# Attention's value product copied out of its accumulator bank by ScalarE, and its PSUM banks shared out anew

## The chip, the cores and the metric

The kernel runs on one core of a Trainium2 chip. The engines are named as in the profile: PE (TensorE; PEld are its weight loads), DVE (VectorE), ACT (ScalarE), POOL (GpSimd) and SP (SyncE, which here only issues transfers). The metric is the device time of one execution in microseconds (us); lower is better. "Clock" is the share of full speed that TensorE was granted.

## The reference, cut to what matters

One post-norm transformer block over x of shape (2, 1024, 512), fp32:

```
q, k, v = split heads of x @ W.T + b + 0.5 * (x @ B.T) @ A.T     # 16 heads of 32, rank 16
attn    = softmax(q @ k.T * 32**-0.5)                            # per batch and head, 1024 x 1024
x       = layernorm(x + lora_linear(attn @ v; Wo, bo, Bo, Ao))
out     = moe(x)      # softmax gate, the best of 8 experts, capacity 256, hidden 704, SwiGLU
shared  = (silu(x @ sw1) * (x @ sw3)) @ sw2
x       = layernorm(x + out + shared)
```

## The kernel before, in words

fp32 products on TensorE are made from a high and a low part (a value cast to a shorter type, and what the cast left out), so that most products consist of three.

The kernel has four stages: the projections (0 to 156 us of the profile), attention (156 to 600), the output projection of the second batch with the shared feed-forward part, and the experts (to 1043). The change lies in attention.

Attention is cut into 16 units u: four heads (of one batch) by half of the queries, so g = u // 2 is the group of four heads. A unit has eight steps, one for each block of 128 keys; step t = 8u + k. The lines below are those of the profile.

- `st_step(t)`: four score matmuls st (L641), one for each head, keys on the partitions, into banks of the PSUM pool `one` (three banks). ACT turns each into an exponential (L650) in a tile pt of SBUF, two heads in one tile of 128 x 1024; the pool `ptp` has PTB of these tiles. After each head stands a list, `between[h]`, of other work.
- `maxima()` makes one of the row maxima that the softmax of a unit needs 12 steps later (LEAD): a matmul s (L203) into a bank of the pool `s1p`, and a DVE reduction of it (L211). The table `S_AT[k][h]` says how many are put into list h of step k, ahead of the other work and behind it. `finish_max` transposes a unit's maxima (L221 mp; ACT L224, DVE L225) and sends them into the tile of queries, where the score matmul subtracts them.
- `av_step(t)`: the product with the values, av (L660), eight steps accumulated in one PSUM bank of the pool `avp` (two banks, so units take turns). At every even t, in list AVQ = 3, stand the av of the two steps before: 16 matmuls. So unit u's last av stands at t = 8(u + 1).
- `adds(t-1)`: the pt tiles of a unit are added up, ahead of the row sums. The table ADDS names what is done at each k: "dd" an accumulating transfer issued by POOL (L678), "pp" additions on POOL, "vv" on DVE (both L681), two of 128 x 1024 each; "pp0" means that tile 0 is added. Units 14 and 15 use DVE.
- `finish(u)` (table FIN): matmuls with ones (L694 sm) give the sums in a bank, ACT copies them (L708 rc), and they go by transfers through DRAM into a small shape r16. `invert(u)` (REC): DVE's reciprocal (L718) and transfers that spread it to rb. Units 14 and 15 take DVE's reciprocal of the sums themselves (L704).
- `normalize(u)` (NRM): part 0, DVE multiplies av by rb in place (L733); part 1, the cast to the high part at_h, on ACT (L738), for units 13 and 14 on DVE (L736); part 2, DVE's low part at_l = av − at_h (L740). For an ordinary unit this stands in step 8(u + 2) + 1, and ends the use of the av bank.
- `add_res(n)` (RES_ADDS): POOL adds the output bias to a block of the residual (L749). `oproj` (OPROJ_AT, L766) is the output projection, of batch 0 between the steps, of batch 1 behind the loop; its first block `op10` takes a bank of `avp`, the others of `s1p` (OP_ONE).

Entries of FIN, REC and NRM are (units later, step k, list); NU − 3 is unit 13. PE, ACT, DVE, POOL and SP run in the order in which the loop issues their work. PSUM's eight banks are shared out as 3 (`one`) + 2 (`avp`) + 3 (`s1p`). The projections use the same pools: `bank1` takes three turns in `one` and one in `avp`, and `fold_w` three blocks in `s1p` and the fourth in `avp`.

Of the kernel before, what the change touches and what calls it, by code (L numbers as in the profile page):

```python
# [9 lines left out]
F32 = mybir.dt.float32  # L10
# [3 lines left out]
ALU = mybir.AluOpType  # L14
AX = mybir.AxisListType
PSUM = bass.MemoryType.PSUM
DRAM = bass.MemoryType.DRAM

P = 128
B, L, D = 2, 1024, 512  # L20
NU = 16
# [3 lines left out]
KC = D // P  # L25
# [5 lines left out]
EPS = 1e-5  # L31
NT = T // P
LEAD = 12
LATE, OP_ONE = (0,), 1
NS = NU * 8
WARM, WCOL = 4, 256
OPER = 4
PTB = 14
OHB = 3
LOADS = {  # L40
    (2, 0): (("k", 0),), (2, 1): (("q", 0),), (2, 3): (("q", 1),),
# [13 lines left out]
AVQ = 3  # L55


FIN = {None: (1, 4, 1), NU - 3: (1, 3, 1), NU - 2: (1, 2, 3)}
REC = {None: (1, 6, 3), NU - 3: (1, 5, 3)}
NRM = {  # L60
    None: ((2, 1, 0), (2, 1, 2), (2, 1, 2)),
    NU - 3: ((2, 0, 1), (2, 0, 1), (2, 0, 1)),
    NU - 2: ((1, 4, 1), (1, 4, 1), (1, 4, 1)),
}


S_AT = (
    ((0, 0), (0, 1), (1, 0), (1, 0)), ((0, 0), (0, 1), (1, 1), (0, 0)),
    ((0, 2), (1, 0), (0, 0), (0, 2)), ((0, 0), (0, 1), (0, 2), (0, 0)),
    ((0, 1), (1, 2), (0, 1), (1, 1)), ((1, 0), (0, 0), (2, 0), (1, 0)),  # L70
    ((0, 0), (1, 0), (0, 1), (1, 0)), ((0, 1), (1, 0), (0, 0), (2, 0)),
)
XTB = 2


ADDS = {
    None: {1: "bb1 dd21", 2: "dd30", 3: "pp4", 4: "pp5", 5: "pp6", 6: "pp0"},
    NU - 2: {1: "bb1 dd01", 3: "dd23 vv4", 4: "vv5", 5: "vv6 vv3", 6: "vv7"},
    NU - 1: {1: "bb1 dd01", 3: "dd23 vv4", 4: "vv5", 6: "vv3"},
}  # L80
OPROJ_AT = (66, 68, 70, 72, 74, 76, 78, 80)
RES_AT = tuple(8 * i + (2 if i % 2 else 6) for i in range(8)) + (70, 74, 86, 90, 100, 102, 106, 110)
RES_ADDS = tuple(t + 3 for t in RES_AT[:14]) + (119, 120)
RB = 2
BTB = 4
AHEAD = 5
# [26 lines left out]
def kernel(  # L113
# [3 lines left out]
    pe, act, dve, pool, sp = nc.tensor, nc.scalar, nc.vector, nc.gpsimd, nc.sync  # L117

    def f(ap):
        return ap.bitcast(F32)  # L120
# [23 lines left out]
    wop = att_right.enter_context(tc.tile_pool(name="wop", bufs=1, side="right"))  # L144
    one_ps = ExitStack()
    one = one_ps.enter_context(tc.tile_pool(name="one", bufs=3, space=PSUM))
    avp = one_ps.enter_context(tc.tile_pool(name="avp", bufs=2, space=PSUM))
    s1p = one_ps.enter_context(tc.tile_pool(name="s1p", bufs=3, space=PSUM))
    wo_h = wop.tile([P, KC, D], F32R, name="wo_h")
    wo_l = wop.tile([P, KC, D], F32R, name="wo_l")  # L150
    Ks = [stk.tile([98, 4, 1024], F32R, name=f"ks{i}") for i in range(2)]
# [11 lines left out]
    def load_k(g, cs=slice(0, 1024), hs=slice(0, 4)):  # L163
        kt = Ks[g % 2]
        for blk, hl in ((0, 0), (1, 1), (2, 0)):
            sp.dma_start(
                out=f(kt[32 * blk : 32 * blk + 32, hs, cs]),
                in_=qk_d[1, g // NG, g % NG, hl].rearrange("(h p) t -> p h t", p=32)[:, hs, cs],
            )
# [13 lines left out]
    def load_q(u, hs=slice(0, 4)):  # L183
        g, qb = u // 2, u % 2
        for blk, hl in ((0, 0), (1, 0), (2, 1)):
            sp.dma_start(
                out=f(Qs[u % 3][32 * blk : 32 * blk + 32, hs]),
                in_=qk_d[0, g // NG, g % NG, hl].rearrange("(h p) t -> p h t", p=32)[
                    :, hs, qb * 512 : qb * 512 + 512
                ],  # L190
            )

    mts, pts, avs, accs, vts = {}, {}, {}, {}, {}
# [40 lines left out]
    with ExitStack() as ph1, tc.manual_schedule(engines=MAN1):  # L234
# [49 lines left out]
            return ba  # L284

        def fold_w(i, ba, k):
            if k == KC - 1:
                lp = avp.tile([P, 512], F32, name=f"lp{i}{k}", tag="av")
            else:
                lp = s1p.tile([P, 512], F32, name=f"lp{i}{k}", tag="s1")  # L290
            pe.matmul(lp, ba[0][:, k * P : k * P + P], ba[1], start=True, stop=True)
            return lp

# [328 lines left out]
    with ph2, tc.manual_schedule(engines={mybir.EngineType.PE}):  # L622
        ptp = att_left.enter_context(
            tc.tile_pool(name="ptp", bufs=PTB, side="left", reuse_waits="tile")
        )
        ap = ph2.enter_context(
            tc.tile_pool(name="ap", bufs=1, side="right", reuse_waits="tile")
        )
# [25 lines left out]
        def av_step(t):  # L654
            u, kc = t // 8, t % 8
            g = u // 2
            if kc == 0:
                avs[u] = avp.tile([P, 512], F32, name=f"av{u}", tag="av")
            for h in range(4):
                pe.matmul(  # L660
                    avs[u][32 * h : 32 * h + 32, :],
                    vts[g][:, kc, 32 * h : 32 * h + 32],
                    pts[t, h // 2][:, h % 2, :],
                    start=kc == 0,
                    stop=kc == 7,
                    skip_group_check=True,
                )

        def adds(t):
            u, kc = t // 8, t % 8  # L670
            for op in ADDS.get(u, ADDS[None]).get(kc, "").split():
                i = u * 8 + int(op[2])
                for pr in range(2):
                    if op[pr] == "b":
                        accs[u, pr] = pts[i, pr]
                    elif op[pr] == "d":
                        to = u * 8 + int(op[3])
                        pool.dma_start(out=pts[to, pr], in_=pts[i, pr], accum_op=ALU.add)  # L678
                    else:
                        eng = dve if op[pr] == "v" else pool  # L680
                        eng.tensor_tensor(accs[u, pr], accs[u, pr], pts[i, pr], ALU.add)  # L681
# [4 lines left out]
        fin = {}  # L686
# [41 lines left out]
        def normalize(u, parts=(0, 1, 2)):  # L728
            g, qb = u // 2, u % 2
            cs = slice(qb * 512, qb * 512 + 512)  # L730
            hi, lo = at_h[:, g % NG, cs], at_l[:, g % NG, cs]
            if 0 in parts:
                dve.tensor_tensor(avs[u], avs[u], fin[u], ALU.mult)  # L733
            if 1 in parts:
                if u in NRM_DVE:
                    dve.tensor_copy(hi, avs[u])  # L736
                else:
                    act.copy(hi, avs[u])  # L738
            if 2 in parts:
                dve.tensor_tensor(lo, avs[u], f(hi), ALU.subtract)  # L740

        def load_res(n):
            b, i = divmod(n, 8)
# [35 lines left out]
        def run(gen):  # L779
            for _ in gen:  # L780
                pass
# [12 lines left out]
        def at_step(table, t, q):  # L794
            for v in range(max(t // 8 - 2, 0), t // 8):
                at = table.get(v, table[None])
                at = at[q] if isinstance(at[0], tuple) else at
                if (v + at[0]) * 8 + at[1] == t:
                    yield v

        for t in range(NS):
            u, k = t // 8, t % 8
            if k == 0:

                if u % 2 == 0 and 2 <= u and u // 2 + 1 < B * NG:
                    for hs in (slice(0, 2), slice(2, 4)):
                        load_k(u // 2 + 1, hs=hs)
                        load_q(u + 2, hs)
                elif u >= 1 and u + 2 < NU:
                    load_q(u + 2)  # L810
                if u % 2 and NG <= u // 2 + 1 < B * NG:
                    load_v(u // 2 + 1)
            if t in RES_AT:
                load_res(RES_AT.index(t))
            between = [[], [], [], []]
            for q in range(4):
                between[q] += [maxima] * S_AT[k][q][0]
            if t + LEAD == NS:
                between[AVQ].append(lambda: finish_max(NU - 1))

            if t and t % 2 == 0:
                between[AVQ].append(lambda: (av_step(t - 2), av_step(t - 1)))
            for v in at_step(FIN, t, 0):
                between[FIN.get(v, FIN[None])[2]].append(lambda v=v: finish(v))
            for q in range(4):
                between[q] += [maxima] * S_AT[k][q][1]
            if t:
                between[AVQ].append(lambda: adds(t - 1))
            for q in range(3):
                for v in at_step(NRM, t, q):  # L830
                    between[NRM.get(v, NRM[None])[q][2]].append(lambda v=v, q=q: normalize(v, (q,)))
            for v in at_step(REC, t, 0):
                if v < RDIR:
                    between[REC.get(v, REC[None])[2]].append(lambda v=v: invert(v))
            if t in RES_ADDS:
                between[3].append(lambda: add_res(RES_ADDS.index(t)))

            if t in OPROJ_AT:
                op0 = oproj(0, OPROJ_AT.index(t), OPER)
                for q in range(3):  # L840
                    between[q].append(lambda q=q, op0=op0: run(op0) if q == 2 else next(op0))
            st_step(t, between)
            for _, fn in [x for x in later if x[0] == 0]:
                fn()
            later[:] = [(n - 1, fn) for n, fn in later if n]
            if t - NS >= OPROJ1:
                next(op10, None)
# [511 lines left out]
```

## Time and profile before

| | before |
|---|---|
| median of 3 runs | 1047.83 us (1046.94 to 1050.71) |
| the profiled execution | 1045.05 us |
| its span, first to last instruction | 1043.3 us |
| mean granted clock of TensorE | 0.991 |
| instructions on PE, DVE, ACT, POOL | 5606, 1156, 985, 404 |
| busy 165 to 563 us (398 long): PE, DVE, ACT, POOL | 396, 316, 258, 337 us |
| busy 576 to 589 us (13 long): PE, DVE, ACT, POOL | 8.4, 7.5, 4.4, 1.5 us; clock 0.74 |

In a row of the timeline stand the start, the duration from first start to last end (a row can hold several instructions, "x8"), the engine, the line, the operation with its tiles, and in brackets the idle time of the engine ahead of it with what released it. In a group's row, busy time and the mean duration in nanoseconds of one instruction stand behind the bar, then the idle time. DMA issues are rows of POOL and SPq. The ends of matmuls are modelled; their starts are recorded.

### The profile page before, as it was taken

What the parts mean: (1) busy time and instruction counts of PE and PEld (TensorE: products, weight loads), DVE (VectorE), ACT (ScalarE), POOL (GpSimd) and SP (SyncE); (2) the same over time, 40 slices, a digit from 0 to 9 for tenths busy, and PEclk for the clock granted to TensorE, in tenths of its full rate; (3) what the DMA queues carried; (4) which work ended last, traced back from release to release, by engine and by line L of the source; (5) the groups of instructions that cost most, each with busy time, mean ns of one, the idle gap of its engine ahead of it and who ended that gap; (6) DMA issues with size and microseconds to landing.
All of it is one profiled execution on the core that took longest, in us unless ns stands there. A gap on an engine that the chain in (4) does not pass through costs nothing. (4 is left out here: it accounts for less than half of the span.)

```text
span 1043.3 us, 15652 instructions
## 1 busy us (share of the span) xinstructions
PE 1016.6 (97%) x5606; PEld 722.7 (69%) x5606; DVE 676.1 (65%) x1156; ACT 520.4 (50%) x985; POOL 536.1 (51%) x404
## 2 busy tenths in 40 slices
PE   8999999999999999999999799999999999999994
PEld 6888784544444456654444279988788899999994
DVE  7732788788878877788877774222253467777752
ACT  5422206666666656576666645222132356555662
POOL 4000006889888977879895155000006056666674
PEclk9999999999999999999999899999999999999998
DMA  9876875686868783587974532000109667777721
GB/s 291 283 230 210 248 211 118 125 186 137 190 134 187 160 181 83 115 168 155 197 163 92 132 104 70 22 21 1 40 1 293 212 198 237 255 244 258 224 82 60
DMA packets 87374, 164.75 MB, mean 158 GB/s; under 512 B 15944, under 2 KB 24648, under 8 KB 87296
## 3 DMA queue, kind: packets, MB, share of 16 engines
q1 hardware_dynamic: 74240, 117.59, 38.8%
q0 software_dynamic: 13056, 46.16, 19.9%
q8 instruction: 44, 0.72, 0.3%
q14 instruction: 34, 0.28, 0.1%
HBM read 96.10 MB, written 33.80 MB: 125 GB/s over the span
## 5 line engine op out<-in xcount | busy, mean ns | idle before, releaser
L211 DVE TENSOR_REDUCE mt<-s 128x1 f32<-128x512 f32 x512 | 318.4, 681 | 75.2 <-PE s L203 75.1
L650 ACT ACTIVATE pt<-st 128x512 f32<-128x512 f32 x512 | 266.3, 618 | 147.5 <-PE st L641 145.6
L681 POOL TENSOR_TENSOR pt<-pt,pt 128x1024 f32<-128x1024 f32 x112 | 264.2, 2387 | 33.4 <-DMA pt<-pt 18.1
L203 PE MATMUL s<-ks,qs 96*128 96x512 f32 x512 | 196.1, 416 | 1.5 <-DVE mt L211 1.0
L641 PE MATMUL st<-qs,ks 98*128 98x512 f32 x512 | 189.3, 417 | 2.7 <-ACT pt L650 1.7
L678 POOL DMA_DIRECT2D pt<-pt x64 | 56.3, 1008 | 195.2 <-PE s L203 164.7
L641 PEld LDWEIGHTS st<-qs,ks 98*128 98x128 f32 x512 | 94.8, 189 | 72.5 <-ACT pt L650 26.8
L203 PEld LDWEIGHTS s<-ks,qs 96*128 96x128 f32 x512 | 94.2, 188 | 72.7 <-DVE mt L211 44.5
L924 PE MATMUL h<-xthe,w13s 128*128 128x256 f32 x704 | 129.9, 283 | 0.0
L924 PEld LDWEIGHTS h<-xthe,w13s 128*128 128x128 f32 x704 | 110.6, 191 | 0.4
L924 PE MATMUL h<-xtle,w13s 128*128 128x256 f32 x352 | 100.2, 285 | 0.0
L912 POOL TENSOR_TENSOR w2s<-w2r,w2s 128x512 fp32r<-128x512 f32 x42 | 65.8, 1588 | 64.9 <-ACT w2s L911 56.3
L1114 POOL DMA_INDIRECT xd_d<-x1a,slot_i x8 | 7.9, 985 | 139.3 <-DVE slot_i L1111 137.2
L660 PE MATMUL av<-pt,vt 128*32 128x512 f32 x512 | 64.0, 613 | 4.3 <-DVE at_l L740 4.3
L924 PEld LDWEIGHTS h<-xtle,w13s 128*128 128x128 f32 x352 | 67.3, 191 | 0.7
L660 PE MATMUL av<-pt,x1b 128*32 128x512 f32 x512 | 61.6, 598 | 0.0
L1010 PE MATMUL y<-w2s,hs 128*128 128x512 f32 x260 | 60.9, 390 | 0.0
L1010 PEld LDWEIGHTS y<-w2s,hs 128*128 128x128 f32 x260 | 48.3, 188 | 10.2 <-DVE hs L992 0.5
L589 DVE TENSOR_TENSOR w13s<-x1a,w13s 128x1024 fp32r<-128x1024 f32 x32 | 47.0, 1468 | 6.5 <-ACT w13s L583 6.5
L345 ACT ACTIVATE oh<-o,bqk_sb 128x512 fp32r<-128x512 f32 x32 | 21.9, 689 | 57.7 <-PE o L330 52.8
L583 ACT CAST w13s<-x1a 128x1024 fp32r<-128x1024 f32 x32 | 33.4, 1044 | 25.6 <-DMA x1a<-in_w_dram 19.4
L330 PE MATMUL o<-xh,wh 128*128 128x512 f32 x116 | 45.3, 391 | 0.0
(567 smaller groups left out, 1699.4 us busy)
## 6 DMA issues: line engine op xcount, KB each, us to landing
pt<-pt POOLq DMA_DIRECT2D x64, 512.0 KB, 7.9
x1a<-in_w_dram SPq DMA_DIRECT2D x32, 512.0 KB, 6.5
w2r<-in_w_dram SPq DMA_DIRECT2D x42, 256.0 KB, 3.2
ks<-qkd SPq DMA_DIRECT2D x36, 256.0 KB, 3.9
qkd<-oh SPq DMA_DIRECT2D x32, 256.0 KB, 2.9
qkd<-ol SPq DMA_DIRECT2D x32, 256.0 KB, 2.5
qs<-qkd SPq DMA_DIRECT2D x30, 256.0 KB, 5.1
qs<-qkd SPq DMA_DIRECT2D x36, 128.0 KB, 6.2
```

Source lines behind the costliest of these rows:

```text
L203: pe.matmul(s1, Qs[u % 3][0:96, h, qt * P : qt * P + P], Ks[g % 2][0:96, h, kh * 512 : kh * 512 + 512], start=True, stop=True,)
L211: dve.tensor_reduce(mts[u][:, c, kh : kh + 1], s1, AX.X, ALU.max)
L330: pe.matmul(o, lhs, rhs, start=k + i == 0, stop=k + i == KC + 1)
L589: (pool if e < 0 else dve).tensor_tensor(lo, raw, f(hi), ALU.subtract)
L641: pe.matmul(sb, Ks[g % 2][:, h, kc * P : kc * P + P], Qs[u % 3][:, h, :], start=True, stop=True,)
L650: act.activation(pts[t, h // 2][:, h % 2, :], sb, AF.Exp, scale=SCALE)
L660: pe.matmul(avs[u][32 * h : 32 * h + 32, :], vts[g][:, kc, 32 * h : 32 * h + 32], pts[t, h // 2][:, h % 2, :], start=kc == 0, stop=kc == 7 ...
L678: pool.dma_start(out=pts[to, pr], in_=pts[i, pr], accum_op=ALU.add)
L681: eng.tensor_tensor(accs[u, pr], accs[u, pr], pts[i, pr], ALU.add)
L912: pool.tensor_tensor(hl[:, 1, :], raw, f(hl[:, 0, :]), ALU.subtract)
L924: pe.matmul(hp[:, j * 256 : j * 256 + 256], lhs, rhs[:, k, :], start=n == 0, stop=n == 11,)
L1010: pe.matmul(o, lhs, rhs, start=n == 0, stop=n == 16)
```

## The change

- `avp` has one bank in place of two, `s1p` four in place of three.
- A new function `av_out(u)` runs in list 3 of step t = 8(u + 1), behind the unit's last av: ACT copies the bank (128 x 512, fp32) to a tile ae of SBUF, of which there are two. It does so for units 0 to 14. `normalize` then works on ae; unit 15 stays in its bank.
- PTB goes from 14 to 13; a pt tile is 4 KB a partition, two ae tiles are 4 KB.
- `S_AT` is a new table. The maxima for each step k were 3, 3, 5, 3, 7, 4, 3, 4 and are 3, 4, 3, 4, 7, 4, 3, 4.
- Unit 13: its reciprocal moves from list 3 to list 1 of the same step, so that it stands ahead of that step's DVE adds; its normalize moves from t = 120 to t = 119, list 3. Unit 14's adds to tile 3 stand one step later, together with those to tile 7. The last two residual adds move from t = 119 and 120 to 114 and 115.
- `op10` and the fourth block of `fold_w` take banks of `s1p`.

ACT has 15 instructions more; the counts of the other engines and the order of SP stay.

```diff
@@ -31,11 +31,11 @@
 EPS = 1e-5
 NT = T // P
 LEAD = 12
-LATE, OP_ONE = (0,), 1
+LATE, OP_ONE = (0,), 0
 NS = NU * 8
 WARM, WCOL = 4, 256
 OPER = 4
-PTB = 14
+PTB = 13
 OHB = 3
 LOADS = {
     (2, 0): (("k", 0),), (2, 1): (("q", 0),), (2, 3): (("q", 1),),
@@ -56,31 +56,31 @@
 
 
 FIN = {None: (1, 4, 1), NU - 3: (1, 3, 1), NU - 2: (1, 2, 3)}
-REC = {None: (1, 6, 3), NU - 3: (1, 5, 3)}
+REC = {None: (1, 6, 3), NU - 3: (1, 5, 1)}
 NRM = {
     None: ((2, 1, 0), (2, 1, 2), (2, 1, 2)),
-    NU - 3: ((2, 0, 1), (2, 0, 1), (2, 0, 1)),
+    NU - 3: ((1, 7, 3), (1, 7, 3), (1, 7, 3)),
     NU - 2: ((1, 4, 1), (1, 4, 1), (1, 4, 1)),
 }
 
 
 S_AT = (
-    ((0, 0), (0, 1), (1, 0), (1, 0)), ((0, 0), (0, 1), (1, 1), (0, 0)),
-    ((0, 2), (1, 0), (0, 0), (0, 2)), ((0, 0), (0, 1), (0, 2), (0, 0)),
-    ((0, 1), (1, 2), (0, 1), (1, 1)), ((1, 0), (0, 0), (2, 0), (1, 0)),
-    ((0, 0), (1, 0), (0, 1), (1, 0)), ((0, 1), (1, 0), (0, 0), (2, 0)),
+    ((2, 0), (0, 0), (1, 0), (0, 0)), ((0, 0), (2, 0), (1, 0), (0, 1)),
+    ((0, 0), (1, 1), (0, 1), (0, 0)), ((0, 0), (1, 1), (0, 1), (0, 1)),
+    ((0, 1), (1, 1), (1, 1), (2, 0)), ((0, 0), (0, 2), (1, 0), (0, 1)),
+    ((0, 1), (1, 0), (1, 0), (0, 0)), ((0, 1), (0, 1), (0, 1), (0, 1)),
 )
 XTB = 2
 
 
 ADDS = {
     None: {1: "bb1 dd21", 2: "dd30", 3: "pp4", 4: "pp5", 5: "pp6", 6: "pp0"},
-    NU - 2: {1: "bb1 dd01", 3: "dd23 vv4", 4: "vv5", 5: "vv6 vv3", 6: "vv7"},
+    NU - 2: {1: "bb1 dd01", 3: "dd23 vv4", 4: "vv5", 5: "vv6", 6: "vv3 vv7"},
     NU - 1: {1: "bb1 dd01", 3: "dd23 vv4", 4: "vv5", 6: "vv3"},
 }
 OPROJ_AT = (66, 68, 70, 72, 74, 76, 78, 80)
 RES_AT = tuple(8 * i + (2 if i % 2 else 6) for i in range(8)) + (70, 74, 86, 90, 100, 102, 106, 110)
-RES_ADDS = tuple(t + 3 for t in RES_AT[:14]) + (119, 120)
+RES_ADDS = tuple(t + 3 for t in RES_AT[:14]) + (114, 115)
 RB = 2
 BTB = 4
 AHEAD = 5
@@ -144,8 +144,8 @@
     wop = att_right.enter_context(tc.tile_pool(name="wop", bufs=1, side="right"))
     one_ps = ExitStack()
     one = one_ps.enter_context(tc.tile_pool(name="one", bufs=3, space=PSUM))
-    avp = one_ps.enter_context(tc.tile_pool(name="avp", bufs=2, space=PSUM))
-    s1p = one_ps.enter_context(tc.tile_pool(name="s1p", bufs=3, space=PSUM))
+    avp = one_ps.enter_context(tc.tile_pool(name="avp", bufs=1, space=PSUM))
+    s1p = one_ps.enter_context(tc.tile_pool(name="s1p", bufs=4, space=PSUM))
     wo_h = wop.tile([P, KC, D], F32R, name="wo_h")
     wo_l = wop.tile([P, KC, D], F32R, name="wo_l")
     Ks = [stk.tile([98, 4, 1024], F32R, name=f"ks{i}") for i in range(2)]
@@ -284,10 +284,7 @@
             return ba
 
         def fold_w(i, ba, k):
-            if k == KC - 1:
-                lp = avp.tile([P, 512], F32, name=f"lp{i}{k}", tag="av")
-            else:
-                lp = s1p.tile([P, 512], F32, name=f"lp{i}{k}", tag="s1")
+            lp = s1p.tile([P, 512], F32, name=f"lp{i}{k}", tag="s1")
             pe.matmul(lp, ba[0][:, k * P : k * P + P], ba[1], start=True, stop=True)
             return lp
 
@@ -666,6 +663,13 @@
                     skip_group_check=True,
                 )
 
+        raws = {}
+
+
+        def av_out(u):
+            raws[u] = ap.tile([P, 512], F32, name=f"ae{u}", tag="ae", bufs=2)
+            act.copy(raws[u], avs[u])
+
         def adds(t):
             u, kc = t // 8, t % 8
             for op in ADDS.get(u, ADDS[None]).get(kc, "").split():
@@ -729,15 +733,16 @@
             g, qb = u // 2, u % 2
             cs = slice(qb * 512, qb * 512 + 512)
             hi, lo = at_h[:, g % NG, cs], at_l[:, g % NG, cs]
+            av = raws.get(u, avs[u])
             if 0 in parts:
-                dve.tensor_tensor(avs[u], avs[u], fin[u], ALU.mult)
+                dve.tensor_tensor(av, av, fin[u], ALU.mult)
             if 1 in parts:
                 if u in NRM_DVE:
-                    dve.tensor_copy(hi, avs[u])
+                    dve.tensor_copy(hi, av)
                 else:
-                    act.copy(hi, avs[u])
+                    act.copy(hi, av)
             if 2 in parts:
-                dve.tensor_tensor(lo, avs[u], f(hi), ALU.subtract)
+                dve.tensor_tensor(lo, av, f(hi), ALU.subtract)
 
         def load_res(n):
             b, i = divmod(n, 8)
@@ -820,6 +825,8 @@
 
             if t and t % 2 == 0:
                 between[AVQ].append(lambda: (av_step(t - 2), av_step(t - 1)))
+                if k == 0:
+                    between[AVQ].append(lambda: av_out(u - 1))
             for v in at_step(FIN, t, 0):
                 between[FIN.get(v, FIN[None])[2]].append(lambda v=v: finish(v))
             for q in range(4):
```

## The prediction

> **What bounds the kernel now.** I read the page first, then the chain of waits, then the timeline of the last attention units and of one ordinary unit.
>
> ```profile
> span 1043.3 us, 15652 instructions
> PE 1016.6 (97%) x5606; PEld 722.7 (69%) x5606; DVE 676.1 (65%) x1156; ACT 520.4 (50%) x985; POOL 536.1 (51%) x404
> L681 POOL TENSOR_TENSOR pt<-pt,pt 128x1024 f32<-128x1024 f32 x112 | 264.2, 2387 | 33.4 <-DMA pt<-pt 18.1 <-ACT pt L650 13.5 <-ACT mh L224 1.2
> ```
>
> TensorE is busy 97% of the span, so the change can gain only where its matmuls start late. POOL's 51% hides that between 165 and 563 us, by the busy time by stretch, it is busy 337 of 398.
>
> ```profile
> PEld s L203 <- DVE mt L211: 44.5, 109, 0.8
> PEld st L641 <- ACT pt L650: 26.8, 110, 0.8
> PE av L660 <- DVE at_l L740: 4.3, 1, 4.3
> ```
>
> The columns are total, count and longest. The first two are weight loads, most of them ahead of a matmul that is not late: where the matmul starts are more than their usual 0.233 apart behind such a wait, the excess in the attention loop sums to 6.3 us for s (a bank not yet reduced) and 4.3 us for st (a bank whose exp has not ended). The third is one single stall, in the timeline:
>
> ```profile
> 560.36 0.58 ACT L708 COPY rc<-sm 128x512 f32<-128x512 f32 x1 [0.97 <-PE sm L694]
> ...
> 568.36 5.26 DVE L681 TENSOR_TENSOR pt<-pt,pt 128x1024 f32<-128x1024 f32 x2 [0.62 <-ACT pt L650]
> 568.38 3.01 POOL L749 TENSOR_TENSOR x1b<-x1b,bo_bc 128x512 f32<-128x512 f32 x2
> ...
> 573.54 0.24 DVE L718 RECIPROCAL r<-r 128x16 f32<-128x16 f32 x1
> 573.71 6.82 DVE L681 TENSOR_TENSOR pt<-pt,pt 128x1024 f32<-128x1024 f32 x6
> ...
> 580.45 0.69 DVE L733 TENSOR_TENSOR av<-av,rb 128x512 f32<-128x512 f32 x1
> ...
> 581.90 0.69 DVE L740 TENSOR_TENSOR at_l<-av,at_h 128x512 fp32r<-128x512 f32 x1
> ...
> 582.64 3.64 PE L660 MATMUL av<-pt,vt 128*32 128x512 f32 x16 [4.32 <-DVE at_l L740]
> ...
> 586.06 1.93 PE L694 MATMUL sm<-pt,ones 128*32 128x512 f32 x8
> ...
> 587.92 1.88 PE L641 MATMUL st<-qs,ks 98*128 98x512 f32 x6
> ```
>
> Unit 15's first av needs the bank of unit 13, which normalize(13) leaves at 582.6, and TensorE waits 4.32. The stretch table adds that the wait costs clock too: full from 563 to 576 and 0.74 from 576 to 589, where av takes 3.64 for its usual 1.92.
>
> ```profile
> 259.97 9.40 POOL L681 TENSOR_TENSOR pt<-pt,pt 128x1024 f32<-128x1024 f32 x4
> 261.99 1.93 PE L660 MATMUL av<-pt,x1b 128*32 128x512 f32 x16
> 263.15 0.69 DVE L733 TENSOR_TENSOR av<-av,rb 128x512 f32<-128x512 f32 x1
> 264.45 1.58 ACT L650 ACTIVATE pt<-st 128x512 f32<-128x512 f32 x3 [1.70 <-PE st L641]
> 264.86 1.89 DVE L211 TENSOR_REDUCE mt<-s 128x1 f32<-128x512 f32 x3 [1.02 <-PE s L203]
> 265.89 0.61 ACT L738 CAST at_h<-av 128x512 fp32r<-128x512 f32 x1
> 266.67 0.68 DVE L740 TENSOR_TENSOR at_l<-av,at_h 128x512 fp32r<-128x512 f32 x1
> ```
>
> This is an ordinary unit (26.54 us, 237.31 to 263.85 by its first matmuls): while POOL runs its adds back to back, the mult and at_l read av in PSUM and keep 0.69.
>
> **The change, part by part.**
>
> *Tail.* The av of unit 15 now needs only the copy of unit 14 (one ACT operation like rc's, 0.58), issued right behind unit 14's last av, two steps earlier. The 4.32 go. With no idle, av and sm should take 1.92 + 1.9 as elsewhere, not the 5.28 between 582.64 and 587.92: about 1.4 more. Together 5.7; bounds 4.3 (the clock drops anyway) and 7. Late next would be unit 14's sums, which need its last add on DVE: the queue is reciprocal, vv5, vv6, vv3, vv7, then normalize(13). The residual adds move to some 559–562, ahead of the dd23 transfers on POOL's queue; those wait for step 115's work at 567.3 anyway, so the transfers are not later, and vv5 no longer meets POOL (4.12 of the 5.26, against 1.21 for such an add alone). The chain can end near 578, sm of unit 14 would start near 580: hidden, by 2 us. SP's queue keeps its order; the reciprocal's transfers (573.8 and 576.4 before) leave some 6 us earlier, and nothing waits for them but normalize(13), which gates no bank any more. What follows in the tail hangs on TensorE's order, so the gain stays.
>
> *Copies.* 15 on ACT at 0.58 are 9 us busy, each as its av ends. ACT is idle 1.70 there (263.92 to 264.45 of it usable before the next exp), so exp starts about 0.1 late; 13 times that is 0 to 1.3, taken as 0.6. Only exps are queued behind, and st behind these.
>
> *The operands in SBUF.* mult and at_l now have two SBUF inputs. What a DVE operation of that kind meets beside POOL is seen in the experts:
>
> ```profile
> 851.07 3.80 POOL L912 TENSOR_TENSOR w2s<-w2r,w2s 128x512 fp32r<-128x512 f32 x3
> ...
> 852.49 3.47 DVE L589 TENSOR_TENSOR w13s<-x1b,w13s 128x1024 fp32r<-128x1024 f32 x1
> ```
>
> It takes 1.21 where POOL rests, and here 3.47: it ends 1.08 after two POOL operations. In a dozen others (1.69 to 1.82) it waits only for the one that runs. Where DVE asked within 0.2 us of the POOL operation's start it lost the next turn too; where it asked 0.55 or more after, it got it. The mults of before ask 0.57 to 2.15 after the start of the running add (2.36 apart), so I expect one wait: 1.03 on average over 13 units, and about 0.3 for at_l. Cover for the mult: DVE is idle 263.84 to 264.86 (1.02), and ACT's cast needs it at 265.89. Behind the mult are the reduces, whom TensorE's s banks wait for; bounds 0 and 13 x 1.33 = 17, taken as 0.2 a unit, 2.6, nearest to the row with the gap of 1.02.
>
> [...]
>
> *POOL and 13 pt tiles.* Each lock also holds POOL's next add, 0.6 to 1.2 a unit, and POOL has 8 x 2.39 of adds + 3.5 of DMA issue + some 5.7 of residual adds and waiting for transfers = 28 at most, 24.5 with overlap, of 26.5. One pt tile fewer makes the exps of steps 2 and 3 wait for pp0, the unit's last add, half a step earlier; in before's times that leaves 0.4 to 2.3 us. A delay of 0.57 eats 0.3 in all units together, one of 1.15 eats 3.5; I take 1.
>
> *Fourth bank, new table.* Matmul counts stay. An s stays late only if four reduces (0.61 each) are outstanding instead of three, and no s pair starts directly behind av in the new table, where DVE and ACT are idle. Bounds: 0 and the 6.3 + 4.3 = 10.6 above; the ordinary unit holds more (64 matmuls x 0.233 + four av and one sm at 1.86 = 24.2, against 26.54), but POOL near its limit would not let it go much below 26. I take 6, 0.45 a unit.
>
> *At nothing.* op10 and the fourth folded weight block in an s bank, four banks to rotate for five in the projections: the distance between uses is four banks, about 11 us, over the 0.7 that ACT takes.
>
> **Sum**: −5.7 + 0.6 + 2.6 + 1 − 6 = −7.5. The profiled execution (1045.05, span 1043.3 and 1.75 around it) would be 1037.5; it lies 2.8 under the median of 1047.83, so 1040.3.
>
> **The rivals.** What can be told from no change is about 0.5%, 5.2 us: below 1042.6 or above 1053.1.
>
> *DVE loses two turns (slower).* If a mult waits one POOL add more, 2.36, it ends near 267.3: the reduces start 2.4 late, ACT's cast 1.4 late with exps behind it; less one matmul for the fourth bank, about 2.2 a unit. Over the 11 units that POOL fills, 24: 1047.83 − 5.7 − 2 + 24 = 1064. It decides once the average wait is above about 2 us. For it: 852.49. Against it: when mults ask. POOL to the end of its chain (some 6 us) would be 3.5 a unit, 1078.
>
> *The small costs eat the table (same).* mult and at_l uncovered by 0.5 a unit (6.5), pt tiles 3.5, copies 1.3, table 5: 1047.83 − 5.7 + 6.3 = 1048. For it: POOL's slack of 2 us. Against: the gap at 263.84.
>
> *The table gives all of 10.6 and the locks stay covered (more)*: 1047.83 − 5.7 − 10.6 + 1 = 1032.5. Against: POOL.
>
> *The tail does not move*, as vv7 is late and sm waits instead: if dd23's transfer lands 3 us later, the stall moves to sm and 4.3 stay: about 1045. For it: in before that chain already ended near 580.
>
> **How the numbers follow.** Forecast 0.45 (1036 to 1045, its own range), more 0.13, tail unmoved 0.06, eaten 0.14, two turns 0.22. The range goes from 1032 (the third rival) to 1064 (the first); beyond lie about half of the third and a third of the first with its 1078, under 2 in 10. Faster: 0.13 + 0.38 of the forecast's 0.45 + a little of the eaten case, 0.54; same: 0.22; slower: 0.22 and a remainder, 0.24.
>
> **What would show it.** Right: the av after 578 starts with no idle and 1.92 long, clock 1.00 from 576 to 589; mult at ordinary units 1 to 2.5 long, with POOL's adds running; the first exp behind each copy 0.1 late; ordinary units at 26.0 to 26.4; s waits halved. Wrong: mults of 3 or more or an at_l of as much, POOL adds above 2.39 on average by more than 0.15, units over 26.6, exps that wait for POOL's pp0, or unit 14's sm waiting for DVE.

## The result and the profile after

The changed kernel takes 1105.48 us (median of 6 runs, 1102.58 to 1108.05) against 1048.08 for the kernel before (6 runs beside it, 1046.2 to 1052.47): a ratio of 1.0541, interval 1.0513 to 1.0569. It is 57 us slower; the forecast was 1040.3, at most 1064. The profiled execution took 1104.38 with a span of 1102.7 and a granted clock of 0.960.

From the page of the changed kernel (line numbers have moved: the mult is L738, POOL's adds L685, exp L647, st L638, av L657):

```profile
span 1102.7 us, 15686 instructions
PE 1033.2 (94%) x5606; PEld 741.3 (67%) x5606; DVE 732.8 (66%) x1156; ACT 529.9 (48%) x1000; POOL 536.7 (49%) x404
L738 DVE TENSOR_TENSOR ae<-ae,rb 128x512 f32<-128x512 f32 x14 | 71.1, 5078 | 8.4 <-DMA rb<-rd 8.2
L685 POOL TENSOR_TENSOR pt<-pt,pt 128x1024 f32<-128x1024 f32 x112 | 263.9, 2380 | 24.6 <-DMA pt<-pt 13.2
```

Fourteen mults hold DVE for 71.1 us, 5.08 each; before, with av in PSUM, they took 0.69. POOL's adds are what they were, 2.38 on average: they lose nothing by the meeting, and DVE pays for it.

The chain of waits of the changed kernel (total, times, longest):

```profile
PEld s L203 <- DVE mt L211: 59.5, 34, 5.7
PE s L203 <- DVE mt L211: 43.1, 10, 5.4
PEld st L638 <- ACT pt L647: 26.0, 40, 4.6
```

Before, TensorE itself waited 1.0 for a reduce in all; now ten stops make 43.1, and an eleventh of 4.2 is put down to an exp that stood behind the cast. The single wait for at_l (4.3 before) is gone. One of the stops, in the timeline:

```profile
270.53 9.35 POOL L685 TENSOR_TENSOR pt<-pt,pt 128x1024 f32<-128x1024 f32 x4
273.56 6.88 DVE L738 TENSOR_TENSOR ae<-ae,rb 128x512 f32<-128x512 f32 x1
274.28 0.59 ACT L671 COPY ae<-av 128x512 f32<-128x512 f32 x1 [1.00 <-PE av L657]
274.76 1.58 ACT L647 ACTIVATE pt<-st 128x512 f32<-128x512 f32 x3
280.36 1.87 DVE L211 TENSOR_REDUCE mt<-s 128x1 f32<-128x512 f32 x3
280.47 0.62 ACT L743 CAST at_h<-ae 128x512 fp32r<-128x512 f32 x1 [4.13 <-DVE ae L738]
281.09 1.39 PE L203 MATMUL s<-ks,qs 96*128 96x512 f32 x2 [4.20 <-DVE mt L211]
283.69 3.64 PE L657 MATMUL av<-pt,x1b 128*32 128x512 f32 x16
```

The mult asks at 273.56, as POOL's second of four adds runs (272.89 to 275.27), and ends at 280.44, 0.56 after the last add (279.88). It waited out the running add and let two more pass. The reduces stand behind it, four s banks fill, ACT makes its copy and three exps and then stands 4.13 at its cast with the other exps behind, and TensorE stops for 4.2. Then it runs at half clock, by the busy time by stretch (PE, PEld, DVE, ACT, POOL, clock, DMA share, GB/s):

```profile
276.00:281.00 5.00, 0.90 (x4) 0.28 (x2) 5.00 (x3) 0.87 (x3) 3.88 (x2) 0.98 1.01 225
281.00:288.00 7.00, 6.91 (x24) 2.69 (x25) 4.22 (x8) 2.76 (x7) 0.12 (x1) 0.53 0.32 72
```

From 281.09 to 287.26 come five matmuls of s and st and one av, which take 5 x 0.233 + 1.85 = 3.0 at full clock and took 6.2. So a stop costs 4.2 + 3.2 in all. Between the first exps of a unit and the next lie mostly 32 to 33 us where it was 26.5; the two units in which POOL's adds met the mult least (mults of 0.78 and 1.71) took 0.3 and 0.1 more than before. The eleven stops account for the loss: attention's last exp ends 57.6 later (657.8 for 600.2), the span is 59.4 longer.

The tail, in contrast, went as forecast:

```profile
640.54 0.59 ACT L671 COPY ae<-av 128x512 f32<-128x512 f32 x1
643.09 1.92 PE L657 MATMUL av<-pt,vt 128*32 128x512 f32 x16
643.62 0.69 DVE L738 TENSOR_TENSOR ae<-ae,rb 128x512 f32<-128x512 f32 x1
644.83 1.04 PE L698 MATMUL sm<-pt,ones 128*32 128x512 f32 x8
645.80 1.66 PE L638 MATMUL st<-qs,ks 98*128 98x512 f32 x6
```

Unit 15's first av starts with no idle time and takes 1.92. From the last transpose of the maxima (mp) to the first matmul of the second batch's output projection it is 32.1 us (629.31 to 661.44), before 39.2 (564.59 to 603.77): 7.0 gained.

### The profile page after: what moved, and what is told of

It is laid out like the page before. It is cut to its first block, busy times and chain, and to the rows that moved or that the text cites. A ratio compares the mean times of both kernels' runs of the same rounds, so it can differ in the third digit from the quotient of the medians.

```text
span 1102.7 us, 15686 instructions
## 1 busy us (share of the span) xinstructions
PE 1033.2 (94%) x5606; PEld 741.3 (67%) x5606; DVE 732.8 (66%) x1156; ACT 529.9 (48%) x1000; POOL 536.7 (49%) x404
## 5 line engine op out<-in xcount | busy, mean ns | idle before, releaser
L647 ACT ACTIVATE pt<-st 128x512 f32<-128x512 f32 x512 | 268.2, 612 | 135.7 <-PE st L638 132.5
L685 POOL TENSOR_TENSOR pt<-pt,pt 128x1024 f32<-128x1024 f32 x112 | 263.9, 2380 | 24.6 <-DMA pt<-pt 13.2
L203 PE MATMUL s<-ks,qs 96*128 96x512 f32 x512 | 196.1, 422 | 43.2 <-DVE mt L211 43.1
L638 PE MATMUL st<-qs,ks 98*128 98x512 f32 x512 | 202.2, 426 | 7.5 <-ACT pt L647 6.6
L203 PEld LDWEIGHTS s<-ks,qs 96*128 96x128 f32 x512 | 101.0, 197 | 84.4 <-DVE mt L211 59.5
L638 PEld LDWEIGHTS st<-qs,ks 98*128 98x128 f32 x512 | 96.7, 197 | 90.3 <-issue 42.2
L738 DVE TENSOR_TENSOR ae<-ae,rb 128x512 f32<-128x512 f32 x14 | 71.1, 5078 | 8.4 <-DMA rb<-rd 8.2
L657 PE MATMUL av<-pt,x1b 128*32 128x512 f32 x512 | 68.8, 660 | 0.0
L657 PE MATMUL av<-pt,vt 128*32 128x512 f32 x512 | 67.8, 645 | 0.0
```

The lines of the kernel that those rows point to most:

```text
L203: pe.matmul(s1, Qs[u % 3][0:96, h, qt * P : qt * P + P], Ks[g % 2][0:96, h, kh * 512 : kh * 512 + 512], start=True, stop=True,)
L638: pe.matmul(sb, Ks[g % 2][:, h, kc * P : kc * P + P], Qs[u % 3][:, h, :], start=True, stop=True,)
L647: act.activation(pts[t, h // 2][:, h % 2, :], sb, AF.Exp, scale=SCALE)
L657: pe.matmul(avs[u][32 * h : 32 * h + 32, :], vts[g][:, kc, 32 * h : 32 * h + 32], pts[t, h // 2][:, h % 2, :], start=kc == 0, stop=kc == 7 ...
L738: dve.tensor_tensor(av, av, fin[u], ALU.mult)
```

## The experiments

The theory after the result: two SBUF inputs make the mult wait, not for one POOL add but for all that POOL has ready (the lock, as it is called below), and everything else follows from that. The rivals: the copies, the single av bank with 13 pt tiles, or the new table. Behind each expectation stand the median of the run with its range, and its ratio to the kernel before, run beside it (medians of 1045.6 to 1047.7), with a 95% interval.

**Normalize moved away from POOL's adds.** The changed kernel with

```diff
-    None: ((2, 1, 0), (2, 1, 2), (2, 1, 2)),
+    None: ((2, 4, 0), (2, 4, 2), (2, 4, 2)),
-OPROJ_AT = (66, 68, 70, 72, 74, 76, 78, 80)
+OPROJ_AT = (70, 72, 74, 76, 78, 80, 82, 84)
```

> The changed kernel, with the three parts of an ordinary unit's normalize moved from step 1 (lists 0 and 2) to step 4 of the same unit (t = 8(u+2)+4), where POOL issues transfers and adds nothing; the output projection of the first batch moves four steps later with it, since it reads the last of these units. Theory (the lock): the mult with two SBUF inputs loses its turn to every POOL add that is queued without a gap, stays 5 to 7 us in DVE, and holds the reduces behind it and with them TensorE. Away from POOL's adds the mult should take 0.7 to 1.8 us, TensorE's eleven stops of 4.7 us and the low clock behind them should go, and the kernel should come to 1032 to 1042 us: before, less about 5.7 of the tail, and less what the fourth bank and the table give (two steps took 5.55 to 5.57 us where undisturbed, against 5.67 to 5.98 before). Rival (copies, the single av bank and 13 pt tiles cost the time): these stay as they are, so the time stays above 1080.

1036.18 us (1035.37 to 1036.27) against 1046.78: 0.9897, interval 0.9880 to 0.9913. One unit of its timeline:

```profile
268.33 3.55 POOL L682 DMA_DIRECT2D pt<-pt  x4
271.70 0.68 DVE L738 TENSOR_TENSOR ae<-ae,rb 128x512 f32<-128x512 f32 x1
273.97 0.61 ACT L743 CAST at_h<-ae 128x512 fp32r<-128x512 f32 x1
275.12 0.67 DVE L745 TENSOR_TENSOR at_l<-ae,at_h 128x512 fp32r<-128x512 f32 x1
275.36 2.69 POOL L685 TENSOR_TENSOR pt<-pt,pt 128x1024 f32<-128x1024 f32 x1 [3.48 <-DMA pt<-pt]
```

The same mult, on the same tiles, takes 0.68 while POOL issues transfers. All fourteen take that (0.681 to 0.684). Here at_l starts just ahead of POOL's first add, and it is the add that is drawn out (2.69). TensorE's wait for reduces falls from 43.1 to 1.2. The kernel is 10.6 us faster than the one before, where the changed one was 57.4 slower: 68 between them. The theory holds, the rivals fall: copies, single bank, 13 tiles and table are all still there.

**The lock alone.** The kernel before, with the copies, normalize on them, and 13 pt tiles; two av banks, old table, old tail:

```diff
-PTB = 14
+PTB = 13
+        def av_out(u):
+            raws[u] = ap.tile([P, 512], F32, name=f"ae{u}", tag="ae", bufs=2)
+            act.copy(raws[u], avs[u])
...
+            av = raws.get(u, avs[u])
-                dve.tensor_tensor(avs[u], avs[u], fin[u], ALU.mult)
+                dve.tensor_tensor(av, av, fin[u], ALU.mult)
```

> The kernel before (two av banks, three s banks, old table, old tail), with only the ACT copies of av to SBUF, normalize on these copies, and 13 pt tiles to pay for them. Theory (the lock): mults of 5 to 7 us at the eleven or so units where POOL adds, a TensorE stop of about 4.9 at each, and the low clock behind it: 1100 to 1120 us. Rival (the single av bank makes TensorE wait for ACT's copy, or the new table starves DVE): there are two banks and the old table here, so 1046 to 1055.

1118.91 (1118.04 to 1119.78), 1.0689 (1.0668 to 1.0710). From its groups:

```profile
L740 DVE TENSOR_TENSOR ae<-ae,rb 128x512 f32<-128x512 f32 x14 | 74.6, 5332 | 3.8 <-DMA rb<-rd 3.8
```

and from its chain of waits:

```profile
PE s L203 <- DVE mt L211: 51.3, 12, 5.8
```

Copies, operands in SBUF and 13 pt tiles by themselves cost 72 us, more than the whole change, whose other parts give some back; the run above has the same copies and tiles without the loss, so the operands' wait is what costs. With three s banks the stops are longer, most 4.9 to 5.2 between matmul starts for 4.6 to 4.9.

**Less of POOL's chain left.** As the first, with normalize at step 2:

```diff
-    None: ((2, 4, 0), (2, 4, 2), (2, 4, 2)),
+    None: ((2, 2, 0), (2, 2, 2), (2, 2, 2)),
```

> The changed kernel with an ordinary unit's normalize at step 2 of its unit (lists 0 and 2) in place of step 1, the output projection of the first batch four steps later as in the run at step 4. At step 2 POOL has some 2.8 us less of its chain of adds left than at step 1. Theory (the mult waits for the end of the chain): mults of 2.5 to 4.5 us in place of 5 to 7, TensorE stops of about 1.5 to 3 in place of 4.7, and 1050 to 1080 us. Rival (the cost does not depend on how much of the chain is left, as if any overlap cost one fixed time): mults of 5 to 7 and about 1105.

1057.59 (1056.63 to 1058.54), 1.0096 (1.0070 to 1.0122). The same unit in its timeline:

```profile
265.74 4.73 POOL L685 TENSOR_TENSOR pt<-pt,pt 128x1024 f32<-128x1024 f32 x2
268.08 2.94 DVE L738 TENSOR_TENSOR ae<-ae,rb 128x512 f32<-128x512 f32 x1
271.06 0.62 ACT L743 CAST at_h<-ae 128x512 fp32r<-128x512 f32 x1 [2.22 <-DVE ae L738]
```

The mult asks just ahead of the last add's start and waits for it to end (270.48). Mults average 2.73, eight of them 2.9 to 3.8 and two longer (4.09 and 5.17), TensorE waits 11.4 for reduces, and the clock stays near full (0.987). The price follows what is left of the chain, as the theory has it.

**What lets DVE in.** Two kernels put something small between POOL's adds.

```diff
                         eng.tensor_tensor(accs[u, pr], accs[u, pr], pts[i, pr], ALU.add)
+                        if eng is pool:
+                            pool.memset(gap, 0.0)
```

> The changed kernel with one thing added: behind each of POOL's adds in attention stands a POOL memset of 128 x 1, which reads nothing in SBUF and takes about 0.1 us. Theory in its finer form (DVE waits for a gap in POOL's reading, not for a turn): the mult gets in at the first memset, so it takes at most one add and 0.7, 0.7 to 3.1 us, mean about 1.8, in place of 5 to 7, TensorE's stops shrink below 1 us, and the time falls to 1040 to 1060. Rival (DVE waits until POOL's whole chain is done, whatever stands in it, as with a lock kept for the queue): mults of 6 and 1105 to 1110 us.

1109.67 (1108.80 to 1110.54), 1.0601 (1.0579 to 1.0622): a miss. From its timeline:

```profile
274.80 2.38 POOL L686 TENSOR_TENSOR pt<-pt,pt 128x1024 f32<-128x1024 f32 x1
275.26 7.17 DVE L741 TENSOR_TENSOR ae<-ae,rb 128x512 f32<-128x512 f32 x1
277.12 0.09 POOL L688 MEMSET gap<- 128x1 f32 x1
277.18 2.37 POOL L686 TENSOR_TENSOR pt<-pt,pt 128x1024 f32<-128x1024 f32 x1
279.50 0.09 POOL L688 MEMSET gap<- 128x1 f32 x1
```

DVE waits through the two memsets that stand between adds (a third follows the last add at 281.83). The second uses a power of 128 x 1 near the end of the chain:

```diff
                         eng.tensor_tensor(accs[u, pr], accs[u, pr], pts[i, pr], ALU.add)
+                        if op == "pp6" or (op == "pp0" and pr == 0):
+                            pool.tensor_tensor(gap, gap, expo, ALU.pow)
```

> The changed kernel with a POOL operation of 128 x 1 (a power, as the layernorm has it, about 0.55 us) put behind three of the adds at the end of POOL's chain (both of pp6, the first of pp0). In the changed kernel the two mults that took 0.78 and 1.71 were those where such an operation followed the running add; the memsets of the other run opened no turn. If such an operation gives DVE its turn: mults of at most 3.1 us, TensorE stops under 1.5, 1045 to 1070 us. If those two were accidents: mults of 5.5 to 7 and 1105 to 1115.

1058.07 (1057.72 to 1058.42), 1.0123 (1.0104 to 1.0142).

```profile
210.48 2.39 POOL L687 TENSOR_TENSOR pt<-pt,pt 128x1024 f32<-128x1024 f32 x1
210.84 2.67 DVE L742 TENSOR_TENSOR ae<-ae,rb 128x512 f32<-128x512 f32 x1 [0.77 <-DMA rb<-rd]
212.84 1.07 POOL L689 TENSOR_TENSOR gap<-gap,expo 128x1 f32<-128x1 f32 x1
213.43 1.87 DVE L213 TENSOR_REDUCE mt<-s 128x1 f32<-128x512 f32 x3
```

Now DVE gets its turn as the running add ends (212.87; the mult ends 0.64 later), and it is the power that is drawn out, 1.07 for 0.56. The mults average 1.75, none above 3.0. The 42 powers keep POOL busy for 31.8 us more, and still the kernel is only 12.5 us slower than the one before, where the changed one was 57.4 slower; where these 12.5 lie was not traced. So it is not a turn for each operation: here DVE waited while adds followed that POOL already had ready, and a memset of 0.09 did not break this (7.17), a power of 0.56 did (2.67). Why one and not the other, the runs do not settle. They do show that the memset leaves no time between the adds (one ends at 277.18, the next starts there), while a power takes 0.56 and did not hold up DVE as it ran (0.69):

```profile
266.80 0.56 POOL L689 TENSOR_TENSOR gap<-gap,expo 128x1 f32<-128x1 f32 x1
267.11 0.69 DVE L742 TENSOR_TENSOR ae<-ae,rb 128x512 f32<-128x512 f32 x1 [0.80 <-DMA rb<-rd]
267.34 2.72 POOL L687 TENSOR_TENSOR pt<-pt,pt 128x1024 f32<-128x1024 f32 x1
```

So the length of the pause between POOL's adds may be what counts, and not the kind of operation. A longer memset was not tried.

**What the rest of the change is worth**, each undone in the kernel with normalize at step 4 (1036.18). The old table S_AT in place of the new, as in the change's diff read backwards:

> The kernel with the late normalize (step 4), with the table S_AT of before in place of the new one; one av bank, four s banks and the copies stay. Reading one (the fourth bank gives the steady gain): the table matters little, an ordinary unit stays at about 25.5 us between its first exps, as with the new table, and the time is within 3 us of 1036. Reading two (the table, made for one more bank, gives it): units go back to about 26.2 to 26.5, and the time is 1041 to 1046.

1036.90 (1034.15 to 1038.71), 0.9904 (0.9882 to 0.9927): no difference beyond the intervals; undisturbed units are 25.9 in place of 25.46, but fewer are longer. Three s banks in place of four, with one bank left idle:

```diff
-    s1p = one_ps.enter_context(tc.tile_pool(name="s1p", bufs=4, space=PSUM))
+    s1p = one_ps.enter_context(tc.tile_pool(name="s1p", bufs=3, space=PSUM))
```

> The kernel with the late normalize (step 4) and the new table, with three s banks in place of four (one of the eight banks is left unused). Reading one (the fourth bank gives the steady gain): units go back to 26.2 to 26.5 us and the time to 1043 to 1048. Reading two (the table): within 3 us of 1036.

1060.51 (1059.68 to 1061.50), 1.0127 (1.0108 to 1.0147). Units take 27.45, two more than with four, and attention starts 5.7 later (161.6 for 155.9), since the projections' weight blocks all take these banks now. The 24 us are the price of taking a bank from the new table, not what the bank is worth: the kernel before, with the old table on three s banks, had undisturbed units of 26.53. The old table on three banks was not run with the late normalize. The last units as before:

```diff
-REC = {None: (1, 6, 3), NU - 3: (1, 5, 1)}
+REC = {None: (1, 6, 3), NU - 3: (1, 5, 3)}
-    NU - 3: ((1, 7, 3), (1, 7, 3), (1, 7, 3)),
+    NU - 3: ((2, 0, 1), (2, 0, 1), (2, 0, 1)),
-    NU - 2: {1: "bb1 dd01", 3: "dd23 vv4", 4: "vv5", 5: "vv6", 6: "vv3 vv7"},
+    NU - 2: {1: "bb1 dd01", 3: "dd23 vv4", 4: "vv5", 5: "vv6 vv3", 6: "vv7"},
-RES_ADDS = tuple(t + 3 for t in RES_AT[:14]) + (114, 115)
+RES_ADDS = tuple(t + 3 for t in RES_AT[:14]) + (119, 120)
```

> The kernel with the late normalize (step 4), with the last units as before: unit 13's reciprocal in list 3 and its normalize at t = 120, unit 14's adds to tile 3 early, the last residual adds at t = 119 and 120. As I predicted for the tail, the copy alone takes away TensorE's stop at unit 15's first av, since the bank is free at once; the edits only move DVE and POOL work that nothing waits for. Expected: within 1.5 us of 1036. Rival (the edits are needed too, since DVE's add vv5 meets POOL's residual adds and unit 14's sums then wait): a stop of 2 to 4 us ahead of unit 14's sm, 1038 to 1041.

1037.45 (1037.00 to 1038.33), 0.9905 (0.9885 to 0.9924): 1.3 more, within the intervals, and no stop ahead of the sums. The same lines the other way round, alone, in the kernel before:

> The kernel before with only the edits at the last units: unit 13's reciprocal in list 1 and its normalize at t = 119, unit 14's adds to tile 3 a step later, the last two residual adds at t = 114 and 115. Two av banks stay, so unit 15's first av still waits for normalize(13). As the prediction had it, vv5 no longer meets POOL and the reciprocal's transfers leave 6 us earlier, so normalize(13) ends at about 579 to 580 in place of 582.6: TensorE's stop there falls from 4.3 to 1 to 2 us, the clock stays full, and the time falls by 3 to 5, to 1043 to 1045. Rival (normalize stays behind the same adds of DVE and the stop stays): 1047 to 1048.

1043.33 (1042.37 to 1045.76), 0.9969 (0.9959 to 0.9978), 3.4 less. The stop shrinks, but in the profiled execution av still takes 3.64 for its usual 1.92:

```profile
579.65 0.69 DVE L740 TENSOR_TENSOR at_l<-av,at_h 128x512 fp32r<-128x512 f32 x1
580.39 3.64 PE L660 MATMUL av<-pt,vt 128*32 128x512 f32 x16 [2.56 <-DVE at_l L740]
```

I expected the stop at 1 to 2 us and full clock; the time fell in the range all the same. The profiled execution took 1045.2, the second longest of the ten, so its rows need not be those of the median.

**Better still?** In the kernel at step 4 some at_l (up to 2.56) meet POOL's first adds, so two placements tried to end normalize earlier. The first:

```diff
-    None: ((2, 4, 0), (2, 4, 2), (2, 4, 2)),
+    None: ((2, 4, 0), (2, 4, 0), (2, 4, 1)),
```

> As the run with normalize at step 4, with its cast on ACT in list 0, right behind the mult, and at_l in list 1, so that both are done before POOL's first add of the unit. In that run at_l asked as POOL's first adds had started in some units, took 1.1 to 2.6 us, and TensorE's s matmuls came 0.34 us apart in place of 0.23 behind it, in units of 26.8 where others took 25.46. Theory (the lock is what is left of the loss): all at_l at 0.7, ordinary units at 25.5, and the time 3 to 6 us below 1036, 1030 to 1033. Rival (those units are long for another reason, waits for pt tiles or transfers): 1035 to 1037.

1038.05 (1037.74 to 1038.98), 0.9932 (0.9920 to 0.9944): a miss. From its chain of waits and its timeline:

```profile
ACT at_h L743 <- DVE ae L738: 17.9, 12, 1.6
```

```profile
352.14 5.15 POOL L685 TENSOR_TENSOR pt<-pt,pt 128x1024 f32<-128x1024 f32 x2 [1.38 <-ACT pt L647]
352.24 2.82 DVE L745 TENSOR_TENSOR at_l<-ae,at_h 128x512 fp32r<-128x512 f32 x1
```

ACT now stands waiting for the mult, and at_l still meets POOL in five units. It ends at 355.06, 0.54 after the first of the two adds, taken as 2.38 long (354.52): here DVE got the next turn. The same with the old table:

> The same with the table S_AT of before. With the old table units took 25.9 where nothing else was late, against 25.46 with the new one, so if the time with normalize at step 4 was equal only because at_l was met differently, this one should now be some 4 us slower than the one with the new table: 1034 to 1037. If the table is worth nothing: within 1.5 us of it.

1037.83 (1035.34 to 1038.80), 0.9926 (0.9912 to 0.9941): the table is again worth nothing. The second placement:

```diff
-    None: ((2, 4, 0), (2, 4, 2), (2, 4, 2)),
+    None: ((2, 3, 3), (2, 4, 0), (2, 4, 0)),
```

> As the run with normalize at step 4, with the mult one list earlier (step 3, list 3) and the cast and at_l both in list 0 of step 4. In the run with the tight placement ACT's cast stood waiting for the mult, 17.9 us in 12 units, with the exps behind it, and at_l met POOL's first adds in five units (1.95 to 2.83 us). Here the mult is done before ACT comes to the cast, and at_l should ask some 0.7 to 1 us earlier, ahead of POOL's first adds: ACT's wait for the mult near 0, all at_l at 0.7, ordinary units at 25.5, 1030 to 1034. Rival (the mult now asks while POOL's last add runs, or units are long for another reason): mults of up to 2 us, or units still at 25.9 and more, 1036 to 1040.

1040.72 (1039.23 to 1041.85), 0.9928 (0.9909 to 0.9946): a miss that tells something. Every mult and at_l now takes 0.68 or 0.69, and it is no faster: 7.0 below the kernel before beside it, where the two tight placements lay 7.5 and 7.7 below theirs and the kernel at step 4 lay 10.6 below. From its chain of waits:

```profile
ACT at_h L743 <- DVE ae L738: 11.4, 12, 1.0
PE mp L221 <- DVE mx L214: 9.2, 11, 2.6
```

ACT waits for the mult once more, and the transpose of the maxima for DVE's last reduction, which now stands behind normalize. What was left of the lock is no longer the bound. The order on ACT and DVE may be, as these two waits suggest; no run tests it. The version with normalize at step 4 remains the best of those run, though with the old table (0.9904) or the old tail (0.9905) it cannot be told from the new.

## Why the prediction was wrong

*Operands in SBUF: the step that failed.* "I expect one wait: 1.03 on average over 13 units", taken as 2.6 us in all, with 17 as the upper bound. Measured: a median mult of 6.19, 71.1 in all for 14 x 0.69 before, and the units from the third on are together 67 us longer. The direction of the contention was read rightly from the experts' rows. What failed was the rule for turns, "where it asked 0.55 or more after, it got it". It holds in the rows it came from, and not in attention. These are rows of the kernel before:

```profile
872.87 1.82 DVE L589 TENSOR_TENSOR w13s<-x1a,w13s 128x1024 fp32r<-128x1024 f32 x1
873.57 1.55 POOL L612 TENSOR_TENSOR sce<-sce,expo 128x1 f32<-128x1 f32 x1
922.33 1.17 ACT L911 CAST w2s<-w2r 128x512 fp32r<-128x512 f32 x2
925.31 1.30 POOL L912 TENSOR_TENSOR w2s<-w2r,w2s 128x512 fp32r<-128x512 f32 x1
926.00 1.69 DVE L589 TENSOR_TENSOR w13s<-x1b,w13s 128x1024 fp32r<-128x1024 f32 x1
926.57 2.28 POOL L912 TENSOR_TENSOR w2s<-w2r,w2s 128x512 fp32r<-128x512 f32 x1
```

Behind the first DVE operation came a power. The second asked 0.69 after a POOL operation's start and got the next turn, though the cast that POOL's next operation needed had ended at 923.50; it is this one that was drawn out, 2.28 for 1.30. The mult at 273.56 asked 0.67 after an add's start and lost both turns that came. So neither when DVE asked nor whether POOL's next operation was ready tells these rows from the adds; what does is not shown.

*The upper bound* counted the rest of one add for each mult (1.03, and 0.3 for at_l), though the row at 852.49 showed two passing. A bound should have taken the wait to the end of POOL's chain: about 6 us, as the rival's last sentence had it.

*The rival "DVE loses two turns"* had mechanism and place right: "POOL to the end of its chain (some 6 us) would be 3.5 a unit, 1078". The size was off by half, for two reasons: TensorE stopped for 4.2, and each stop cost 3.2 more at half clock. The prediction had read this very price in before's tail (clock 0.74) and not carried it over. With 4.2 + 3.2 − 1.1 (what an undisturbed unit gains) = 6.3 over eleven units, less 7 of the tail, the sum gives 1048 + 62 = 1110; measured 1105. The rows at 568.36 and 852.49, in which DVE lost a turn, spoke for it, those like 926.00 against, and it was given 0.22.

The runs show the wait itself, 0.68 beside transfers against a median of 6.19 beside adds, and that it is for more than the running operation: up to three further POOL operations (the mult at 578.07, which ended at 584.35) went ahead of a DVE operation that was already waiting.

*Tail.* Predicted 5.7, bounds 4.3 to 7; measured 7.0. The clock's part was counted only up to 587.92, as 1.4; a clock of 0.74 over the 13 us from 576 is 3.4, less what fell into the stop itself. That the copy does it and the edits at the last units add little is shown: 1.3 us with the copies there (within the intervals), 3.4 of the 7 without them.

*Copies.* 0.59 each, right. The first exp behind the copy follows its st by 0.62 where it was 0.60; in two units, those of the mults of 0.78 and 1.71, by 1.34 for 0.54, and these two grew by 0.3 and 0.1. So little or nothing of the 0.6 was paid.

*POOL and 13 pt tiles.* Taken as 1. That a DVE operation holds POOL's next one is seen in the experts (the power at 873.57, 1.55 for the 0.55 of the one at 875.44). But in the changed kernel POOL's adds did not lengthen at all (2.38), since DVE did all the waiting. The sign named for it, exps that wait for POOL, came in the kernel with normalize at step 4: eight exps wait 8.0 us in all for POOL's adds, at most 1.3 each, and none did before. How much of that reached TensorE is open; its own wait for exps went from 1.7 to 3.0.

*Fourth bank, new table.* Taken as 6 together, 0.45 a unit. Without the lock an undisturbed unit is 1.07 shorter (25.46 for 26.53), though from attention's first exp to unit 15's only 2.7 us remain of it (414.7 for 417.4), since other units got longer. With four banks the choice of table makes no difference in time; with three, the new table is slower than the kernel before. So the gain goes with the bank, but how much the bank gives with the old table alone was not separated.

*At nothing.* Attention's first exp comes 0.6 earlier than before (155.7 for 156.3): right, as long as there are four s banks.

*The sum without the lock* was −7.5 with 2.6 for it, so some −10; the kernel without it measured −10.6. That is partly luck: up to unit 15's first exp that kernel gained 3.0 (570.6 for 573.7) where 0.6 + 1 − 6 = −4.4 was counted, and the tail gave 1.3 more than counted.

## What to carry to other kernels

Before an operand of a DVE operation is moved from PSUM to SBUF, look at what POOL does at that time: the mult took 0.69 from PSUM, and with two SBUF inputs beside back-to-back POOL adds a median of 6.19, since it waited here for the end of the chain, not for one operation. Put such an operation where POOL issues transfers (0.68 here) or idles (0.69 at 643.62); moving it by three steps turned a loss of 57 us into a gain of 10.6. And price a stop of TensorE of some 4 us at nearly twice its length, for the clock behind it: here 4.2 cost 3.2 more, at a granted clock of 0.53.

## What was not expected of the hardware

- POOL's adds kept their place against a waiting DVE operation for up to three turns: the mult at 578.07 asked while an add ran (576.84 to 579.23), and an add and two residual adds (579.19 to 583.80) went ahead of it; it ended at 584.35. With the lock alone the longest mult took 8.02, for 6.88 here. DVE got in where the next POOL operation was a power of 128 x 1 (the wait then ended as the running add did, at 212.87), ahead of an add in the first tight placement (at_l, 352.24 to 355.06), and ahead of an operation of 128 x 512 in the experts of the kernel before (926.00). A memset of 0.09 did not let it in. Where the line runs is open: at 852.49 in the kernel before, POOL's next operation was released by a cast (852.01 to 852.64) that ended after DVE had asked, and it still went ahead; at 926.00 the cast had ended 2.50 before DVE asked, and DVE went ahead.
- POOL issuing transfers did not hold up DVE: in the kernel at step 4 all fourteen mults took 0.68, among them the one at 271.70, beside DMA issues from 268.33 to 271.88.
- Less idle time than in a stop of the change was followed by a low clock: in the kernel at step 4 TensorE was busy 1.54 of the 3.00 us from 557 to 560, and the granted clock was 0.59 from 560 to 564. In the run at step 2 it was busy 3.54 of the 4.00 us from 295 to 299 and 3.88 of the 5.00 from 299 to 304, and the clock stayed at 1.00 in both.
